# Conv, Fourier mixing and FFN on one core: merged reordering transfers, a depthwise unit on VectorE, packed sums over h

## Chip, core and metric

One core of a Trainium2 chip runs the whole batch of 32 images in one launch. The metric is the device time in microseconds; the profile is one execution of the same program. TensorE (PE) multiplies, VectorE (DVE), ScalarE (ACT) and GpSimd (POOL) do elementwise work, and SyncE (SP) issues every DMA of the steady state.

## Reference

For each of 32 images `x` (56 x 56 pixels, 96 channels, f32):

```python
# layer 0: an inverted bottleneck whose weights are mixed per image from four experts
rw = sigmoid(mean(x, (1, 2)) @ Wr + br)                      # 4 mixing weights of this image
h = relu(bn(x @ (rw . Wpw) + rw @ bpw))                      # 96 -> 384 channels
h = relu(bn(sum_e rw[e] * (depthwise3x3(h, Wdw[e]) + bdw[e])))
x = bn(h @ (rw . Wpwl) + rw @ bpwl) + x                      # 384 -> 96, shortcut
# layer 1, on tokens t = x as (3136, 96)
h = relu(bn(layernorm(t) @ w1.T))                            # 96 -> 192
X = fft(h, axis=tokens, norm="ortho")                        # over all 3136 tokens
y = ifft(relu(X.re*rd - X.im*id + rb) + 1j*relu(X.im*rd + X.re*id + ib)).real
t = t + bn(y @ w2.T)
t = t + ffn(layernorm(t))       # 96 -> 384 -> 96, operands in 8 bits (e5m2), sums in f16
```

## The kernel before

**Work of an image.** An image lives in two half tiles `xh[0]`, `xh[1]` (96 channels plus a row of ones, 30 rows w of 58), each in a ring of three places. Stages, with the names that the profile uses:

- *Mixing.* ACT sums each half; `pooled`, a small matmul with `wr_s` and a sigmoid give `mix`. DVE then mixes `wk` (expansion), `small` (depthwise taps and biases) and `wkc` (projection). `wkc` goes through DRAM (`wd`) into `wk2`, which has every fourth channel in each 32-partition quadrant.
- *Conv.* A half has three units of 128 channels, so an image has six. In a unit the depthwise 3x3 runs on PE in 32x32 tiles: pixels are split by parity, four parities and 8 channels make 32 rows, and a 32x32 matrix from `wg` (built by POOL) has the taps. Four groups g of 32 channels are expanded (4 matmuls `ps<-x,wk` each, one per pixel parity), ACT writes each group with a ReLU to `h`, and four DMAs `hp<-h` per group put channel and parity in the order that the tiles want: 16 DMAs of 54.4 KB per unit. The conv itself is 64 matmuls `ps<-hp,wg` on 16 tiles; ACT adds the bias, four DMAs `h<-hp` of 196 KB reorder back, and the projection (16 matmuls `ps<-h,wk` per unit, 32 rows each) ends with DVE adding to `xh`.
- *Fourier, forward.* Strips of 14 rows: transposes and `bn_stats` for the layernorm (`ln`), the matmul with `w1c` (`ps<-w1c,x`), the scaling `ha` on DVE, and the sums over h, `ps<-ha,da`: for each of 7 row pairs one matmul of 116 x 116 x 192. The two rows of a pair lie 58 partitions apart, and the matrix `da` (loaded for each strip, two DMAs of 178 KB) is half zeros: each row meets its own 58 columns only. ACT copies the result to `g`, two DMAs write it to DRAM `gd`.
- *Fourier, middle and back.* After all four strips, seven groups of frequencies: load `g2` (shown as `g<-gd`), transform over w (`ps<-dftb_s,g`), the complex ReLU on ACT and DVE (`za`, `zb`, `tmp`), `w2` (`ps<-w2a,za`, `ps<-w2b,zb`), the inverse over w (`ps<-zo,dftc_s`), `y`, and out to DRAM `yd`. Then per strip `yt` and `dd` are loaded and summed back over h (`ps<-dd,yt`).
- *FFN.* Per strip: layernorm in 8 bits (`nt`, turned with `pick8`: `ps<-pick,nt`), `fw1`, `fw2`, the sum into `xh`, and four DMAs per image to the output.

**Order.** Every steady-state instruction is first recorded as an `Op` with an engine, an estimated duration, a due time and the buffers that it reads, writes or takes. `Plan.order` plays these through, engine by engine, and emits them in that order; on the chip each engine keeps it. The due times repeat by `PERIOD`. Three images overlap: one in the conv, one in the Fourier stage, one behind it. Durations and lags of the plan are constants of the code, not measurements.

All instructions of the steady state go through one wrapper, `Pinned.issue`, so the profile shows them with one line, L261 before. They are told apart by their tiles.

Of the kernel before, what the change touches and what calls it, by code (L numbers as in the profile page):

```python
# [18 lines left out]
NE = 4  # L19
# [10 lines left out]
TP = 2 * (S + 2)  # L30
# [7 lines left out]
NG = 12  # L38
NSTK = 9 * NC3 + 2 * NC3 + 1
# [97 lines left out]
class Op:  # L137
    __slots__ = ("eng", "dur", "due", "emit", "bufs", "takes", "left", "ready", "after", "end", "seq")
# [3 lines left out]
LAG = {"PE": 0.25, "DVE": 0.12, "ACT": 0.2, "POOL": 0.2, "SP": 2.3}  # L142
SAME = {"PE": 0.0, "DVE": 0.06, "ACT": 0.05, "POOL": 0.05, "SP": 2.3}


class Plan:
# [5 lines left out]
    def add(self, eng, dur, due, emit, reads=(), writes=(), takes=()):  # L152
        op = Op()
        op.eng, op.dur, op.due, op.emit = eng, dur, due, emit
        op.takes = list(takes)
# [25 lines left out]
    def order(self):  # L181
# [3 lines left out]
        events, n = [], 0  # L185
        done = []
# [10 lines left out]
        def start(op, now):  # L197
            for b in op.takes:
                b.got = b.ring.take(b.n)
            op.end = now + op.dur  # L200
            free[op.eng] = op.end
            done.append(op)
            push(op.end, "end", op)
# [20 lines left out]
        while events:  # L224
            now = events[0][0]
            while events and events[0][0] <= now:
# [3 lines left out]
                elif kind == "end":  # L230
                    for a in x.after:
                        a.left -= 1
                        lag = SAME[x.eng] if a.eng == x.eng else LAG[x.eng]
                        a.ready = max(a.ready, now + lag)
                        if a.left == 0:
                            push(a.ready, "ready", a)
                    push(now + (2.3 if x.eng == "SP" else 0.15), "give", x)
                else:
                    for b in x.bufs:
                        b.users -= 1  # L240
                        if b.users == 0:
                            b.ring.give(b.got)
# [24 lines left out]
def kernel(  # L267
# [35 lines left out]
    xr = [ring(3, [C + 1, HW + 2, S + 2], F32, f"x{h}_") for h in range(2)]  # L303
# [26 lines left out]
    stk16 = const([128, NE + 1, 16 * NG + NG + 1], F32, "stk16")  # L330
# [11 lines left out]
    for p in range(2):  # L342
        nc.vector.tensor_copy(pick8[:, S * p : S * p + S], ident[:TP, (S + 2) * p : (S + 2) * p + S], saturate=False)
# [25 lines left out]

    with tc.tile_pool(name="prep", bufs=1) as pp:  # L370
# [8 lines left out]
        nc.vector.tensor_reduce(of_pixel, half.rearrange("p (r s) -> p s r", s=4), AX.X, ALU.add)  # L379
        raw = temp([128, 4, 27 * NE], "raw")  # L380
# [13 lines left out]
        for q in range(4):  # L394
            nc.sync.dma_start(rawb[q::4], stk[:, 30:33, :].rearrange("(g r) k e -> g r (k e)", r=4))
            nc.sync.dma_start(v2b[q::4], vecs[:, lo : lo + 12].rearrange("(g r) k -> g r k", r=4))
        row_s = temp([128, NROWS], "row_s")
# [19 lines left out]
        nc.sync.dma_start(dftb_s, dftb)  # L417
# [40 lines left out]
        bn_scale(s2b, v2b[:, :, 0:3], v2b[:, :, 9:12], EPS_CONV)  # L458
        s3 = temp([128, 1], "s3")
# [38 lines left out]
        bn_shift(stk16[:, NE, 17 * NG : 17 * NG + 1], vec("b3"), vec("m3"), s3, "sh3")  # L498

# [42 lines left out]
    r_h = places(4, [128, 15 * (S // 2 + 1)], F32, "h")  # L542
    r_hp = places(3, [128, 4, 15 * (S // 2 + 1)], F32, "hp")
# [3 lines left out]
    r_small = places(2, [128, 17 * NG + 1], F32, "small")  # L547
    r_mix = places(2, [128, NE + 4], F32, "mix")
    r_ones = places(2, [C, 128], F32, "pooled")
    r_wkc = places(1, [128, NC3, C], F32, "wkc")  # L550
    r_wk2 = places(1, [128, 4, NC3, C], F32, "wk2_")
    r_da = places(2, [TP, SQ, PA], F32, "da")
# [4 lines left out]
    r_g = places(2, [PA, 4, CH], F32, "g")  # L557
# [3 lines left out]
    r_tmp = places(4, [128, 5, 2, S], F32, "tmp")  # L561
# [9 lines left out]
    r_gd = ring(2, [PA, NQ, CH], F32, "gd", dram)  # L571
# [7 lines left out]
    add = plan.add  # L579
# [10 lines left out]
    PERIOD = 130.0  # L590

    def tokens(xb, w):
        at = w * (S + 2) + 1
        return xb.ap[0:C].rearrange("c w h -> c (w h)")[:, at : at + TP]

    def record(b):
# [6 lines left out]
        for h in range(2):  # L603
# [3 lines left out]
            else:  # L607
                add(
                    "SP", 3.0, t0 - 40, lambda h=h: x_dma(sy, b, h),
# [40 lines left out]
        def mix_wk2():  # L650
# [17 lines left out]
        add(  # L668
            "SP", 0.3, t0 + 8, lambda: sy.dma_start(wd.ap, wkc.ap.rearrange("p c o -> p (c o)")),
            reads=[(wkc, 0)], writes=[(wd, 0)], takes=[wd],  # L670
        )
        for s in range(4):
            add(
                "SP", 0.3, t0 + 12,
# [7 lines left out]

        for h in range(2):
            hid = [Buf(r_h2) for _ in range(NC3)]
            for c in range(NC3):
                due = t0 + (h * NC3 + c) * PERIOD / (2 * NC3)
                wg, hp = Buf(r_wg), Buf(r_hp)

                def weights(c=c, wg=wg):
                    shape = [128, 16, 8, 4]  # L690
                    m = mask.rearrange("p (t c q) -> p t c q", t=1, q=1).to_broadcast(shape)
                    t = small.ap[:, 64 * c : 64 * c + 64].rearrange("p (t c q) -> p t c q", c=1, q=4)
                    po.tensor_tensor(
                        wg.ap.rearrange("p g k (c q) -> p (g k) c q", q=4), m, t.to_broadcast(shape), ALU.mult
                    )

                add("POOL", 1.1, due - 12, weights, reads=[(small, 0)], writes=[(wg, 0)], takes=[wg])
                for g in range(4):
                    hg, ps = Buf(r_h), Buf(banks)
                    at = due - 10 + g * PERIOD / (8 * NC3)  # L700
                    chan = 128 * c + 32 * g

                    def expand(h=h, ps=ps, chan=chan):
                        for s in range(4):
                            pw, ph = divmod(s, 2)
                            te.matmul(
                                ps.bank()[32 * s : 32 * s + 32, 0:435],
                                wk.ap[:, chan : chan + 32],
                                xh[h].ap[:, pw : pw + 29 : 2, ph : ph + 57 : 2],
                                start=True, stop=True,  # L710
                            )

                    add(
                        "PE", 0.95, at, expand, reads=[(wk, 0), *((xh[h], k) for k in (0, 1, 2))],
                        writes=[(ps, 0)], takes=[ps, hg],
                    )
                    add(
                        "ACT", cols("ACT", 435), at + 1,
                        lambda ps=ps, hg=hg: se.activation(hg.ap, ps.bank()[:, 0:435], AF.Relu),
                        reads=[(ps, 0)], writes=[(hg, 0)],  # L720
                    )
                    for r in range(4):
                        add(
                            "SP", 0.1, at + 2,
                            lambda g=g, r=r, hg=hg, hp=hp: sy.dma_start(
                                hp.ap[32 * r : 32 * r + 32, g, :], hg.ap[r::4, :]
                            ),
                            reads=[(hg, 0)], writes=[(hp, (g, r))], takes=[hp] if g == r == 0 else [],
                        )
                ps = Buf(banks, 4)  # L730

                def conv(wg=wg, hp=hp, ps=ps):
                    for k in range(4):
                        bw, bh = divmod(k, 2)
                        for r in range(4):
                            at = slice(32 * r, 32 * r + 32)
                            for g in range(4):
                                te.matmul(
                                    ps.bank(r)[32 * g : 32 * g + 32, 0:TH],
                                    wg.ap[at, g, k, :],  # L740
                                    hp.ap[at, g].rearrange("p (w h) -> p w h", w=15)[:, bw : bw + 14, bh : bh + 28],
                                    start=(k == 0), stop=(k == 3),
                                )

                add(
                    "PE", 2.9, due, conv,
                    reads=[(wg, 0), *((hp, (g, r)) for g in range(4) for r in range(4))],
                    writes=[(ps, r) for r in range(4)], takes=[ps],
                )
                for r in range(4):  # L750
                    add(
                        "ACT", cols("ACT", TH), due + 1,
                        lambda c=c, r=r, ps=ps, hp=hp: se.activation(
                            hp.ap.rearrange("p g n -> p (g n)")[:, TH * r : TH * r + TH], ps.bank(r)[:, 0:TH], AF.Relu,
                            bias=small.ap[:, 16 * NG + 4 * c + r : 16 * NG + 4 * c + r + 1],
                        ),
                        reads=[(ps, r), (small, 0)],
                        writes=[(hp, ("out", r)), *((hp, (g, k)) for g in range(4) for k in range(4))],
                    )
                for q in range(4):  # L760
                    add(
                        "SP", 0.1, due + 3,
                        lambda q=q, hp=hp, to=hid[c]: sy.dma_start(
                            to.ap[32 * q : 32 * q + 32].rearrange("p r n -> p (r n)"),
# [531 lines left out]
```

## Time and profile before

| | |
|---|---|
| median of 3 runs | 5353.63 us (5351.17 to 5355.15) |
| the profiled execution | 5352.85 us |
| its span, first to last instruction | 5351.1 us |
| granted TensorE clock, mean | 0.924 |
| pitch of images (start of `pooled`, 956 to 5001 us) | 161.8 us |
| first expanding matmul | 66.9 us |
| DMA per image | 24 MB, 30 thousand packets |

In a line of groups, `ps<-hp,wg 32*32 32x392 f32 x24576 | 1068.8, 596 | 303.7 <-DMA hp<-h 282.9` means: matmuls that write PSUM from `hp` with weights `wg`, on a tile of 32 x 32, 32 partitions of 392 f32 elements, 24576 of them; busy 1068.8 us in all, 596 ns each; the engine idled 303.7 us before them, most of it until a DMA into `hp` landed. An f32 matmul of the code is two instructions on PE. Matmuls on different tiles of the array overlap, so one's duration is no measure of the rate; where that matters the text takes the step from one start to the next. PEclk is the granted clock in tenths of the full one.

### The profile page before, as it was taken

What the parts mean: (1) busy time and instruction counts of PE and PEld (TensorE: products, weight loads), DVE (VectorE), ACT (ScalarE), POOL (GpSimd) and SP (SyncE); (2) the same over time, 40 slices, a digit from 0 to 9 for tenths busy, and PEclk for the clock granted to TensorE, in tenths of its full rate; (3) what the DMA queues carried; (4) which work ended last, traced back from release to release, by engine and by line L of the source; (5) the groups of instructions that cost most, each with busy time, mean ns of one, the idle gap of its engine ahead of it and who ended that gap; (6) DMA issues with size and microseconds to landing.
All of it is one profiled execution on the core that took longest, in us unless ns stands there. A gap on an engine that the chain in (4) does not pass through costs nothing.

```text
span 5351.1 us, 133311 instructions
## 1 busy us (share of the span) xinstructions
PE 4688.6 (88%) x52802; PEld 2974.9 (56%) x52802; DVE 2612.8 (49%) x8867; ACT 2305.4 (43%) x4618; POOL 1210.3 (23%) x1236
## 2 busy tenths in 40 slices
PE   3898898989898899998889988898988898988986
PEld 1555555555565565555555555565555555655665
DVE  3244554454554454554454544454544444544545
ACT  2234443444543344544344543444544444434443
POOL 1111222222222222222222222122222122221223
PEclk8898999999999999999999999999999899999987
DMA  5666666666666666666666666666666666666652
GB/s 110 136 144 134 141 154 141 154 153 148 150 154 144 149 150 150 149 154 144 151 152 148 148 153 141 150 150 152 145 148 146 148 143 141 153 140 153 148 126 74
DMA packets 964628, 771.78 MB, mean 144 GB/s; under 512 B 654594, under 2 KB 861250, under 8 KB 964002
## 3 DMA queue, kind: packets, MB, share of 16 engines
q1 hardware_dynamic: 964002, 763.25, 63.8%
q8 instruction: 415, 6.80, 0.6%
q14 instruction: 211, 1.73, 0.1%
HBM read 274.71 MB, written 162.99 MB: 82 GB/s over the span
## 4 chain that ended last, share of the span: by engine, by line
PE 51%; DMA 15%; DVE 10%; SPq 6%; ACT 5%; issue 2%; POOL 1%; ACTq 0%; POOLq 0%; DVEq 0%
PE ps L261 51%; DMA hp<-h 7%; SPq L261 6%; DVE ln L261 4%; DMA h<-hp 2%; DVE nt L261 2%; ACT h L261 2%; DVE tmp L261 1%; ACT tmp L261 1%; DVE za L261 1%; DMA x<-in_x_dram 1%; POOL ln L261 1%; DMA da<-in_dfta_dram 1%; DMA out_dram<-x 1%; DMA gd<-g 1%
## 5 line engine op out<-in xcount | busy, mean ns | idle before, releaser
L261 PE MATMUL ps<-hp,wg 32*32 32x392 f32 x24576 | 1068.8, 596 | 303.7 <-DMA hp<-h 282.9
L261 PEld LDWEIGHTS ps<-hp,wg 32*32 32x32 f32 x24576 | 547.2, 113 | 774.5 <-DMA hp<-h 505.9
L261 ACT ACTIVATE hp<-ps,small 128x392 f32<-128x392 f32 x768 | 409.6, 588 | 1177.3 <-PE ps L261 1177.3
L261 PE MATMUL ps<-x,wk 97*32 97x435 f32 x6144 | 731.2, 574 | 46.2 <-ACT n L261 25.4
L261 POOL TENSOR_TENSOR wg<-mask,small 128x512 f32<-128x512 f32 x192 | 205.5, 1070 | 2202.2 <-PE ps L261 2012.7
L261 ACT ACTIVATE h<-ps 128x435 f32<-128x435 f32 x768 | 409.0, 533 | 567.7 <-PE ps L261 504.0
L261 PE MATMUL ps<-h,wk 32*96 32x392 f32 x6144 | 564.0, 495 | 2.0 <-DMA h<-hp 1.2
L261 DVE TENSOR_SCALAR h<-h,fb 128x784 f16<-128x784 f16 x384 | 177.5, 469 | 777.1 <-ACT h L261 775.9
L261 DVE SCALAR_TENSOR_TENSOR x<-ps,small,x 96x392 f32<-96x392 f32 x256 | 148.5, 622 | 728.0 <-PE ps L261 728.0
L261 POOL CAST h<-h 128x784 fp8e5<-128x784 f16 x384 | 328.2, 859 | 581.4 <-DVE h L261 581.4
L261 PEld LDWEIGHTS ps<-h,wk 32*96 32x96 f32 x6144 | 286.9, 158 | 253.2 <-issue 202.4
L261 PE MATMUL ps<-dftb_s,g 112*128 112x112 f32 x2816 | 412.1, 285 | 12.7 <-DMA g<-gd 12.2
L261 PEld LDWEIGHTS ps<-dftb_s,g 112*128 112x128 f32 x2816 | 365.6, 195 | 96.3 <-issue 77.6
L261 ACT CAST h<-ps 128x784 f16<-128x784 f32 x384 | 305.5, 815 | 241.4 <-PE ps L261 235.9
L261 PE MATMUL ps<-ha,da 116*116 116x192 f32 x1792 | 396.6, 376 | 7.7 <-ACT tmp L261 6.4
L261 POOL TENSOR_TENSOR ln<-ln,mhalf 116x7 f32<-116x7 f32 x256 | 394.3, 1540 | 21.3
L261 PEld LDWEIGHTS ps<-ha,da 116*116 116x116 f32 x1792 | 346.2, 210 | 68.8 <-ACT g L261 28.6
L261 PE MATMUL ps<-w1c,x 96*116 96x192 f32 x1792 | 334.1, 330 | 11.6 <-ACT h L261 11.5
L261 DVE BATCH_NORM_STATS2 ln<-ps 116x6 f32<-116x96 f32 x1792 | 315.7, 249 | 41.0 <-PE ps L261 41.0
L261 DVE SCALAR_TENSOR_TENSOR ha<-ps,ln,nshift 116x192 f32<-116x192 f32 x896 | 307.9, 409 | 33.9 <-POOL ln L261 33.3
L261 DVE TENSOR_SCALAR nt<-ps,ln 116x96 fp8e5<-116x96 f32 x896 | 267.0, 370 | 100.9 <-POOL ln L261 100.9
L261 PEld LDWEIGHTS <-fw 128*96 128x96 fp8e5 (+1 forms) x1536 | 151.3, 112 | 281.2 <-issue 233.3
(152 smaller groups left out, 6301.1 us busy)
## 6 DMA issues: line engine op xcount, KB each, us to landing
hp<-h SPq DMA_DIRECT2D x3072, 54.4 KB
h<-hp SPq DMA_DIRECT2D x768, 196.0 KB
da<-in_dfta_dram SPq DMA_DIRECT2D x256, 177.6 KB
dd<-in_dftd_dram SPq DMA_DIRECT2D x128, 355.2 KB
gd<-g SPq DMA_DIRECT2D x128, 336.0 KB
g<-gd SPq DMA_DIRECT2D x192, 224.0 KB
x<-in_x_dram SPq DMA_DIRECT2D x64, 609.0 KB
yt<-yd SPq DMA_DIRECT2D x128, 294.0 KB
```

The lines of the kernel that those rows point to most:

```text
L261: return self.tc.keep_in_program_order(method(*args, **kwargs))
```

## The change

1. **Transfers merged by unit.** `h` becomes a tile of a whole unit (four groups side by side; two places instead of four smaller ones), and four DMAs of 223 KB per unit take the place of sixteen `hp<-h`. The ring of `hp` has two places instead of three. All four groups must be ready before the first DMA, and the conv waits for all four DMAs.
2. **One of six units on VectorE** (half 0, chunk 2). Its channels are expanded 128 at a time (4 matmuls over 1740 columns), ACT applies the ReLU into `hv` and starts the accumulator with the middle tap and the bias, DVE adds the other eight taps (8 `scalar_tensor_tensor` of 128x784 on each of two quarter images, so 16 in all), ACT ends with a ReLU. No DMA, no `wg`. Its projection is 4 matmuls of 128 rows with `wkc`, which gets a second place.
3. **Sums over h in 64x64 tiles.** The two rows of a pair now lie 64 partitions apart (rows of `xh` are 64 wide), and `da` keeps only the 58 used columns, 64 apart. Four row pairs are 16 half-size problems, 8 matmuls on four tiles per group of up to four pairs; a group of three computes one pair twice. The packed matrix `dad` is made once at the start, on DVE from `dfta`, and lies in DRAM; a strip loads 91 KB twice from it. `gd` has another layout.
4. **The plan.** A DMA is now an issue of 0.45 us on SP and a transfer with its size on a shared queue (1.7 us and 0.22 MB per us); `PERIOD` is 125 instead of 130; some durations differ (conv 2.9 to 4.3). Every engine's order comes out new.

```diff
-LAG = {"PE": 0.25, "DVE": 0.12, "ACT": 0.2, "POOL": 0.2, "SP": 2.3}
+LAG = {"PE": 0.25, "DVE": 0.12, "ACT": 0.2, "POOL": 0.2, "SP": 0.2}
+DMA_LAG, DMA_RATE = 1.7, 2.2e5
...
+    def move(self, size, due, emit, **keys):
+        return self.add("SP", 0.45, due, emit, size=size, **keys)
...
+            if op.eng == "SP" and op.size:
+                nonlocal moved
+                moved = max(moved, op.end + DMA_LAG) + op.size / DMA_RATE
+                push(moved, "end", op)
...
-    r_h = places(4, [128, 15 * (S // 2 + 1)], F32, "h")
-    r_hp = places(3, [128, 4, 15 * (S // 2 + 1)], F32, "hp")
+    r_h = places(2, [128, 4 * 15 * HWP], F32, "h")
+    r_hp = places(2, [128, 4, 15 * HWP], F32, "hp")
-    r_wkc = places(1, [128, NC3, C], F32, "wkc")
-    r_da = places(2, [TP, SQ, PA], F32, "da")
+    r_wkc = places(2, [128, NC3, C], F32, "wkc")
+    r_da = places(2, [128, SQ, 64], F32, "da")
...
-    PERIOD = 130.0
+    PERIOD = 125.0
+    BY_VECTOR = ((0, DC),)
...
+        def by_vector(h, c, due, acc):
+            hv = Buf(r_h)
+            edges = (0, 8, 16, 23, 30)
...
+                    te.matmul(
+                        ps.bank()[:, 0 : n * (S + 2)], wk.ap[:, 128 * c : 128 * c + 128],
+                        xh[h].ap[:, edges[i] : edges[i + 1], 0 : S + 2], start=True, stop=True,
+                    )
...
+            def first(i):
+                src, to, w = taps(i, 4)
+                se.activation(to, src, AF.Identity, scale=w, bias=small.ap[:, NSM + 9 : NSM + 10])
+            def one(i, tap):
+                src, to, w = taps(i, tap)
+                ve.scalar_tensor_tensor(to, src, w, to, ALU.mult, ALU.add)
+            def last(i):
+                to = taps(i, 4)[1]
+                se.activation(to, to, AF.Relu)
...
-                    for r in range(4):
-                        add(
-                            "SP", 0.1, at + 2,
-                            lambda g=g, r=r, hg=hg, hp=hp: sy.dma_start(
-                                hp.ap[32 * r : 32 * r + 32, g, :], hg.ap[r::4, :]
+            for r in range(4):
+                move(
+                    223000, due - 10,
+                    lambda r=r: sy.dma_start(
+                        hp.ap[32 * r : 32 * r + 32].rearrange("p g n -> p (g n)"), hg.ap[r::4, :]
...
-                    "PE", 2.9, due, conv,
+                "PE", 4.3, due, conv, reads=[(wg, 0), *((hp, r) for r in range(4))],
...
+                if plain[c]:
+                    v = hid[c].ap.rearrange("p r n -> p (r n)").rearrange("p (w h) -> p w h", h=S)
+                    for q in range(4):
+                        qw, qh = pixel(q)
+                        te.matmul(
+                            ps.bank(q)[0:C, 0:TH], wkc.ap[:, c, :], v[:, qw::2, qh::2], start=False, stop=True,
+                        )
...
-                        da.ap[(S + 2) * p : (S + 2) * p + S], dfta[S * p : S * p + S, st * SQ : st * SQ + SQ, :]
+                        da.ap[XW * p : XW * p + S, :, 0:KR], dad[S * p : S * p + S, st * SQ : st * SQ + SQ, :]
...
-                    for q in range(nq):
-                        te.matmul(
-                            ps.pair[:PA, 256 * q : 256 * q + CH], da.ap[:, q0 + q, :],
-                            ha.ap[:, q, :], start=True, stop=True,
-                        )
+                    for t in range(2):
+                        for j in range(2):
+                            q = min(2 * t + j, nq - 1)
+                            for p in range(2):
+                                at = slice(XW * p, XW * p + S)
+                                te.matmul(
+                                    ps.pair[64 * j : 64 * j + 64, 512 * p + 256 * t : 512 * p + 256 * t + CH],
+                                    da.ap[at, q0 + q, :], ha.ap[at, q, :], start=True, stop=True,
+                                )
...
+        for i in range(2):
+            nc.sync.dma_start(big, dfta[:, i * (NQ // 2) : (i + 1) * (NQ // 2)])
+            for q in range(NQ // 2):
+                nc.vector.tensor_scalar_mul(to[:, q], v[:, q, :, 0], par[:PB, 0:1])
+                nc.vector.scalar_tensor_tensor(to[:, q], v[:, q, :, 1], par[:PB, 1:2], to[:, q], ALU.mult, ALU.add)
+            nc.sync.dma_start(dad[:, i * (NQ // 2) : (i + 1) * (NQ // 2)], small_a)
```

## The prediction

> **What bounds the kernel now.** I read the page's first three parts, then the waits, then one conv unit in the timeline, then the steady stretch by windows.
>
> ```profile
> PE 4688.6 (88%) x52802; PEld 2974.9 (56%) x52802; DVE 2612.8 (49%) x8867; ACT 2305.4 (43%) x4618; POOL 1210.3 (23%) x1236
> ...
> q1 hardware_dynamic: 964002, 763.25, 63.8%
> ...
> L261 PE MATMUL ps<-hp,wg 32*32 32x392 f32 x24576 | 1068.8, 596 | 303.7 <-DMA hp<-h 282.9
> ...
> L261 PE MATMUL ps<-ha,da 116*116 116x192 f32 x1792 | 396.6, 376 | 7.7 <-ACT tmp L261 6.4
> ```
>
> TensorE (PE) is the bound: 88% busy, the others at half or less, and 51% of the chain that ended last. Its largest group, the conv, is also the one it waits for longest: 303.7 us before it, 282.9 of them for the transfers `hp<-h`.
>
> ```profile
> 2588.79 6.71 SPq L261 DMA_DIRECT2D hp<-h  x8
> 2589.38 0.85 PE L261 MATMUL ps<-hp,wg 32*32 32x392 f32 x6
> 2595.25 2.60 PE L261 MATMUL ps<-hp,wg 32*32 32x392 f32 x39 [5.02 <-DMA hp<-h]
> ```
>
> This timeline shows such a wait: the conv starts, stops after 6 matmuls, and stands 5.02 us until pieces of `hp` land, while the DMA-issuing queue (SPq) spends 6.71 us on eight issues. One `hp<-h` issue takes 592 ns at the median and there are 3072; all DMA issues together take 3566 us of SPq, 111 us per image.
>
> ```profile
> 956.00:5001.00 4045.00, 3627.76 (x41258) 2295.41 (x41255) 2008.43 (x6803) 1797.89 (x3602) 935.32 (x950) 0.93 0.66 148
> ```
>
> The columns are the window, busy PE, PEld, DVE, ACT, POOL, clock, DMA share, GB/s. It holds 25 image pitches (starts of `pooled`, 956 to 5001 us): **161.8 us per image**, of which PE is busy 145.1. The clock is 0.93 because PE runs at half clock for 813 us of the span, in spells of 3.4 to 10 us that begin in or just behind the longer PE gaps (the 5.02 us gap above lies in one of 6.8 us). A stall is paid twice: as idle time, and as half speed after it.
>
> The profiled execution took 5352.85 us, its span 5351.1; the median of the runs is 5353.63, so the sum needs no rescaling.
>
> **The change, part by part, per image.** The dependences can be followed in the order of instructions of both kernels. I counted the PE work that the order puts between two points, at undisturbed durations of this trace.
>
> *One unit leaves the conv.* An undisturbed unit takes 3.66 us of PE (5th percentile of 192): −3.7. Its 16 expanding matmuls (3.6 us) become 4 over 1740 columns in all. A full-array f32 row steps 163 ns per 192 columns (`ps<-w1c,x`), two instructions a matmul: 1740 × 0.85 ns × 2 = 3.0, −0.6. Its projection is 4 full matmuls instead of 16 quarter ones: 8 × 333 = 2.7 against 2.9, taken as 0. Sum −4.2.
>
> *The other five units stop waiting.* From a conv instruction to the next PE instruction the steps add up to 41.8 per image; six undisturbed units are 22.0. So 19.8 are stall and half clock. In the order of before, the PE work between a unit's last expanding matmul and its conv is 5.5, 6.9, 3.0, 10.2, 4.6 and 6.8 us; in the changed order 12.9, 7.0, 12.8, 11.6 and 11.0. The need: four issues replace sixteen, the data is 891 KB in packets of 6960 B, which the trace lacks. Nearest is `h<-hp`, 803 KB in 6272 B packets on the same 32-partition pattern: 5.5 us (median) from first to last packet, the first 1.1 us after the issue. Scaled: 0.55 (ACT) + 0.6 + 1.1 + 6.1 = 8.4 us on a free queue. Four of five units are covered with 2.6 to 4.5 us to spare, one is 1.4 short. I leave 3 of the 19.8 and book −16.8; bounds −10 (queueing eats the spare) and −19.8.
>
> Merging does not make the bytes cheaper. A 1740 B packet took 93 ns on the mean, a 6272 B one 589: 18.6 against 10.6 B/ns. The five merged units send 5 × 128 × 32 = 20480 packets in the run; at 650 ns (589 scaled by bytes) over 16 engines that is 832 us, where all six units now cost 574. `h<-hp` loses a sixth of 905 (−151), `da` becomes 100352 packets of 232 B at about 21 ns (132) instead of 14336 of 3248 B at 197 (176), and 2560 fewer DMAs save some 34 of closing 4 B writes. Together +30 on 3450 us: DMA work stays at 108 to 109 us per image.
>
> The rows give 146 GB/s for such a group (803 KB in 5.5 us), and they are used. The Trainium skill is of two minds here ("SBUF — State Buffer"): its section The DMA setup-cost knee wants the largest single transfer, its section Door 1: The DMA port swizzle says that 32 partitions reach half the ports, some 218 GB/s at best. By the page 891 KB would take 4.1 us and a fixed 2, an estimate; that would spare the short unit 1 us and leave the sum 1 us per image lower.
>
> *SPq.* 120 issues of 0.6 us become 40: 111 falls to about 60 us per image. It is what lets SPq be on time; counted in the wait above.
>
> *Sums over h.* 56 instructions at 172 ns are 9.7, with half clock 11.7 (steps per image). After: 4 strips × 16 matmuls × 2 = 128 instructions on 64x64 tiles. If four tiles run at once (32x96 row tiles do: 78 ns per 392-column instruction, where one alone takes 327), 41 ns each: 5.2. Gain −6.0. If they do not overlap, 128 × 163 = 20.9: +9.2. The first is nearer to three other tiled groups here.
>
> *VectorE (DVE).* 16 multiply-adds of 128x784. The rows `small<-stk,mix,small` (205 columns, 434 ns) and `wk<-wpw_s,mix,wk` (384, 619) rise by 1.03 ns per column; carried on from `wk`, 784 columns take 1.03 us, and from `tmp<-za,tmp` (224, 385 ns) 0.96: 16.0 us per image. DVE goes from 80.3 to 96.3 of the pitch and is still not the bound. The order leaves 51.6 us of PE work between this unit's expansion and its projection; hidden. But DVE is in order, and each new step can hold up the normalization behind it, for which PE waits today (79.8 us before `ps<-pick,nt`, 38.5 before `ps<-w2b,zb`, 3.7 per image). One step more in front of such a wait is 1 us; I book +3, bounds 0 and +8.
>
> ```profile
> L261 DVE SCALAR_TENSOR_TENSOR tmp<-za,tmp x224: 374/385/1764, 247.5 to 5281.1; 128x224 f32<-128x224 f32 x96, 128x280 f32<-128x280 f32 x16
> ```
>
> Minimum, median, maximum: a 385 ns step has stretched to 1764, and 90 of the 224 began while a POOL instruction ran (539 ns on the mean). POOL is busy 37 us per image, so of 16 steps some five meet it, at 0.15 to 0.3 us: about 1 us on DVE, inside the +3. If each of five stretched like the longest row (1.38 us over the median) it would be 7, inside the upper bound. The Trainium skill names a cause that speaks against this part ("SBUF — State Buffer", Who interferes with whom): a DVE instruction with two inputs in SBUF and a GpSimd one that reads SBUF exclude each other for a whole instruction. By it every meeting would cost half a POOL instruction or more, which the mean of 539 ns does not show.
>
> *Shorter covers.* From the last backward transform over q to the first over h the order left 12.8 us of PE work, now 8.3, for a DVE copy (0.57), an issue, `yd`, another issue, `yt`; PE waits 11.3 us in all for it now. I book +1 (0 to +3). Conv to projection gains (5 to 9.4), and needs 2.4 (ACT) + 1.1 + 5.5: +0.5.
>
> *ACT* gains 1.0 (5.5 us for the new unit against 4.5) and 0.7 (copies of `g` always 768 wide) on 72: at half load, nothing. *Half clock elsewhere*: fewer spells, −1.5.
>
> *Preparation.* The matrix of the sums is packed on DVE: 56 steps of 58 columns, about 0.2 us (`stk<-wide,s2f` has 173 ns), 11 us ahead of the first mixing step, with a second load behind the first half and a few more loads: +18 once (10 to 30).
>
> **Sum.** 161.8 − 4.2 − 16.8 − 6.0 + 3 + 1.5 − 1.5 = **137.8 us per image**. 24.0 × 31 images (the last one drains on latencies) = 744; 5353 − 744 + 18 = 4627, rounded to **4625 us**. As a check: the PE steps in the order, all undisturbed, add to 121.8 before and 114.0 after, so 40.0 us per image are lost today and 23.8 in the forecast.
>
> **The rivals.**
> *The DMA queue becomes the bound.* 109 us of packets in 138 is 79%, against 66% now, and one queue serves all in turn. If the 6960 B packets take the 785 ns that 6272 B ones take in the middle of a burst (20480 × 785 / 16 = 1005 us instead of 832), it is 114 us, and half the conv stall remains. Pitch about 148: 4930. Against it: the order puts most transfers 10 us ahead.
> *The tiles do not overlap*, so the packed matrix does not do what it says: 137.8 + 15.2 = 153, about 5100.
> *DVE sets the pace*: its lock at the upper bound and chain waits of 8: 144, about 4810.
> *Slower than before.* `hp` has two places instead of three, and a conv needs the whole unit. If landings take so long that every conv waits, nothing hides it. Break-even is 24 us per image back, 4.8 per unit beyond what is booked: landing 16 us behind the last expanding matmul, twice the 8.4. With 20 it is 5 × 9 = 45: pitch 180, some 5950 us. Needed is a queue that is nearly full; 79% speaks against it.
>
> **How the numbers follow.** Forecast 0.62, DMA bound 0.15, DVE 0.10, tiles 0.06, slower 0.06, no difference 0.01. Runs spread by under 0.1%; about 0.2% is what a measurement can tell from no change. Faster 0.93, same 0.01, slower 0.06. The low end takes the conv stall wholly away, no DVE price and two more us of half clock away: 130, 4385. The high end reaches the DMA case: 4920.
>
> **What would show it.** Right: idle time before `ps<-hp,wg` under 100 us and its busy time near 160 × 4 = 640 us; clock above 0.95; `ps<-ha,da` 64x192 below 220 us; DVE near 3130 us busy; DMA share near 80%; first expanding matmul near 85 us. Wrong: conv waits on `hp<-h` above 200 us (queue), `ps<-ha,da` above 500 us (tiles), new long waits of PE on DVE `nt` or `zb` (DVE order), or a pitch that none of these explains.

## The result: slower by 4.6%

| | before | after |
|---|---|---|
| median of 4 runs | 5352.77 us (5351.17 to 5355.15) | 5599.41 us (5594.63 to 5606.10) |
| the profiled execution, its span | 5352.85, 5351.1 us | 5596.55, 5594.7 us |
| granted TensorE clock, mean | 0.924 | 0.88 |
| pitch of images 5 to 25 (starts of `pooled`) | 160.9 us | 169.1 us |
| PE at half clock | 813 us | 1345 us |

The ratio is 1.0461, with a 95% interval from 1.0443 to 1.0479. The forecast was 4625 us, with a range up to 4920: the kernel was to become faster, and it became slower.

These are the lines of the page after that answer to those shown of before, with the vector unit's steps and the sums over h (groups: busy us, mean ns of one | idle us before them and what ended it).

```profile
PE 4414.9 (79%) x49474; PEld 2762.0 (49%) x49474; DVE 3122.6 (56%) x9445; ACT 2338.2 (42%) x4619; POOL 1197.0 (21%) x1204
...
q1 hardware_dynamic: 946154, 687.80, 63.6%
...
PE 47%; DMA 26%; DVE 12%; ACT 7%; issue 3%; SPq 3%; POOL 2%; ACTq 0%; POOLq 0%; DVEq 0%
...
L277 PE MATMUL ps<-hp,wg 32*32 32x392 f32 x20480 | 887.4, 653 | 597.5 <-DMA hp<-h 595.6
...
L277 DVE SCALAR_TENSOR_TENSOR h<-h,small,h 128x784 f32<-128x784 f32 x512 | 514.7, 1045 | 41.0 <-ACT h L277 38.1
```

PE is less busy than before, in a longer span: the work did get less. The conv has fewer matmuls and waits twice as long for `hp<-h` (597.5 us against 303.7), and a quarter of the chain is now DMA. And yet the queue's share, 63.6% of 16 engines, is what it was before. By the page DMA has a third of its time to spare.

The chain of waits in one stretch of the profile after (start, length, what) shows where it stands:

```profile
2741.78 0.68 issue
2742.46 0.65 ACT h L277
2743.11 9.20 DMA hp<-h
2752.45 7.81 PE ps L277 x128
...
2763.50 15.67 PE ps L277 x133
2779.38 13.83 DMA hp<-h
2793.25 8.94 PE ps L277 x128
```

For two convs in a row the chain runs through 9.20 and 13.83 us of transfer, from the first issue to the landing; PE stands idle for 6.76 and 13.05 us of them. SP's own timeline, for the time before the second wait:

```profile
2762.07 3.13 SPq L277 DMA_DIRECT2D h<-hp  x4
2765.30 0.54 SPq L277 DMA_DIRECT2D out_dram<-x  x1
2765.94 8.21 SPq L277 DMA_DIRECT2D gd<-g  x4
2774.24 3.15 SPq L277 DMA_DIRECT2D da<-dad  x2
2777.48 1.81 SPq L277 DMA_DIRECT2D dd<-in_dftd_dram  x1
2779.38 3.36 SPq L277 DMA_DIRECT2D hp<-h  x4
```

Four issues of `gd<-g` hold SP for 8.21 us, and the issues of `hp<-h` stand behind them in order: ScalarE had finished writing `h` at 2766.83 us, 12.5 us before the first of them. One line of the tile `g` in each kernel, before and then after (minimum/median/maximum ns of an issue), shows that long issues of `gd<-g` are the rule:

```profile
L261 SPq DMA_DIRECT2D gd<-g x512: 239/318/1683, 161.2 to 5224.1; - x171
```

```profile
L277 SPq DMA_DIRECT2D gd<-g x512: 227/1510/5007, 165.9 to 5456.9; - x171
```

The same number of issues became almost five times as long at the median. Part of that is their shape: half of the issues of before write only four rows, and 512 issues of 64 rows (e1 below) have a median of 625 ns. The prediction has no term for this transfer.

### The profile page after: what moved, and what is told of

Read it like the earlier page. It is cut to its first block, busy times and chain, and to the rows that moved or that the text cites. A ratio compares the mean times of both kernels' runs of the same rounds, so it can differ in the third digit from the quotient of the medians.

```text
span 5594.7 us, 122771 instructions
## 1 busy us (share of the span) xinstructions
PE 4414.9 (79%) x49474; PEld 2762.0 (49%) x49474; DVE 3122.6 (56%) x9445; ACT 2338.2 (42%) x4619; POOL 1197.0 (21%) x1204
## 3 DMA queue, kind: packets, MB, share of 16 engines
q1 hardware_dynamic: 946154, 687.80, 63.6%
## 4 chain that ended last, share of the span: by engine, by line
PE 47%; DMA 26%; DVE 12%; ACT 7%; issue 3%; SPq 3%; POOL 2%; ACTq 0%; POOLq 0%; DVEq 0%
PE ps L277 47%; DMA hp<-h 13%; DMA g<-gd 4%; DMA out_dram<-x 4%; DVE h L277 3%; DVE ln L277 3%; DMA x<-in_x_dram 2%; SPq L277 2%; POOL ln L277 2%; DVE x L277 1%; DMA dd<-in_dftd_dram 1%; ACT h L277 1%; DMA gd<-g 1%; ACT tmpa L277 1%; DVE ha L277 1%
## 5 line engine op out<-in xcount | busy, mean ns | idle before, releaser
L277 PE MATMUL ps<-hp,wg 32*32 32x392 f32 x20480 | 887.4, 653 | 597.5 <-DMA hp<-h 595.6
L277 PE MATMUL ps<-x,wk 97*32 97x435 f32 (+2 forms) x5376 | 708.9, 586 | 22.7 <-DVE tmpa L277 14.9
L277 DVE SCALAR_TENSOR_TENSOR h<-h,small,h 128x784 f32<-128x784 f32 x512 | 514.7, 1045 | 41.0 <-ACT h L277 38.1
L277 ACT ACTIVATE h<-ps 128x435 f32<-128x435 f32 (+2 forms) x768 | 400.1, 539 | 240.0 <-PE ps L277 211.6
L277 POOL TENSOR_TENSOR ln<-ln,mhalf 120x7 f32<-120x7 f32 x256 | 390.3, 1525 | 21.3
L277 PE MATMUL ps<-w1c,x 96*120 96x192 f32 x1792 | 352.7, 338 | 29.7 <-ACT h L277 21.6
L277 DVE TENSOR_SCALAR nt<-ps,ln 120x96 fp8e5<-120x96 f32 x896 | 267.2, 372 | 175.4 <-POOL ln L277 174.3
L277 DVE SCALAR_TENSOR_TENSOR ha<-ps,ln,nshift 120x192 f32<-120x192 f32 x896 | 310.6, 411 | 82.2 <-PE ps L277 50.3
L277 ACT ACTIVATE tmpa<-ps,fa 128x224 f32<-128x224 f32 (+1 forms) x448 | 223.3, 498 | 256.5 <-PE ps L277 208.7
L277 PEld LDWEIGHTS ps<-w1c,x 96*120 96x120 f32 x1792 | 288.9, 187 | 82.1 <-ACT h L277 41.7
L277 DVE BATCH_NORM_STATS2 ln<-ps 120x6 f32<-120x96 f32 x1792 | 319.1, 253 | 9.7 <-PE ps L277 9.5
```

The source lines that it names most:

```text
L277: return self.tc.keep_in_program_order(method(*args, **kwargs))
```

## The theories

**A: two engines.** The change to `gd` (part 3 of the change) also alters the shape of the write. Before, `gd<-g` was cut into 112 and 4 partitions; after, each write covers the 58 used columns, `g.ap[64 * j : 64 * j + KR]`. The packet records of the trace have no engine number, but they have starts and ends. Counted from them, the time in which so many packets of `gd<-g` were under way (e1 to e3 are the experiments below):

| kernel (packet size) | 1 at once | 2 | 3 | 4 and more |
|---|---|---|---|---|
| after, 58 partitions (1536 B) | 223 us | 1382 | 172 | 6 |
| e1, 64 partitions (1536 B) | 72 us | 34 | 18 | 359, of it 249 at 12 to 17 |
| e2, 58 partitions (3072 and 2304 B) | 414 us | 1419 | 84 | 1 |
| e3, 29 partitions (1536 B) | 3038 us | 196 | 0 | 1 |

So a write of 58 rows goes out on two engines, one of 29 on one, one of 64 on all sixteen (ends are modelled, hence a few more at once than there are engines). 52064 packets of 67.8 ns on two engines are 52064 × 67.8 / 2 = 1765 us each. All packets together are 3592 us per engine on the mean, of which `gd<-g` is 221; the rest, 3371, comes on top if it is even: 5136 us on these two engines, 92% of the span, where the mean over 16 says 63.6%. This is an estimate, and a low one, since the rest is not even. The loads of `dd` have 116 rows, and in before and in e1 their packets are four at a time for most of their time (473 us and 478 us; more than five for under 5). Their 169 us on the mean are then 675 on each of four engines. If the two are among these, they carry some 5640 us, the whole span.

The same count speaks for it: after, the packets of `dd` are two at a time for 372 us, where before has 30 and e1 38, so two of the four lag behind. Taking packets of all kinds, after has one or two under way for 951 us, e1 for 238. A transfer that is spread over all engines, `hp<-h` above all, ends when its part on those two has ended.

The Trainium skill states the rule ("DMA: Bandwidth & Descriptors", Why a DMA increments its semaphore by 16 and not by 1): a DMA is shared out over the largest number of engines up to 16 that divides the size of its slowest dimension on both sides, and for a DMA that SyncE issues they are the lowest-numbered ones. The table agrees: 58 is 2 × 29, 29 is prime, 64 is 4 × 16. The numbers of the two engines the records don't show; that `dd` lags on two of its four fits their always being the same.

**B: merging and order.** Four large issues that need a whole unit, two places of `hp` and a new plan make the conv late, with or without `gd<-g`; this is the rival "Slower than before" of the prediction by itself.

## Experiments

**e1: 64 rows.** The write covers 64 partitions, six of them unused, and moves 10% more bytes.

```diff
-    r_gd = ring(2, [KR, S, CH], F32, "gd", dram)
+    r_gd = ring(2, [64, S, CH], F32, "gd", dram)
...
-                            g.ap[64 * j : 64 * j + KR, 0:nt].rearrange("k t p m -> k t (p m)"),
+                            g.ap[64 * j : 64 * j + 64, 0:nt].rearrange("k t p m -> k t (p m)"),
```

> The changed kernel, with the writes of g to DRAM on 64 partitions instead of 58 (six rows of zeros more; gd gets 64 rows). Order, number of DMA issues and everything else are the same. Theory A (two engines: a DMA over 58 partitions runs on 2 of the 16 DMA engines, 58 = 2 x 29, and these two, with 1765 us of gd packets each besides an even share of 211 us per 1/16 of the rest, are full): over 16 engines the packets cost about 243 us each, SP's issues of gd<-g fall from 1.78 us on the mean back to 0.35, the conv's waits for hp<-h fall from 597 us to under 150, and the time is what the forecast had, 4600 to 4800 us. Theory B (the merged unit transfers, with two places of hp, or the new order themselves make the conv wait): unchanged within 2%, 5500 to 5650 us.

4770.99 us (4760.48 to 4779.07); 0.8936 of before, 0.8918 to 0.8954. From the page of e1, and its line of `gd<-g`:

```profile
PE 4266.3 (89%) x49474; PEld 2673.2 (56%) x49474; DVE 3118.7 (65%) x9445; ACT 2340.3 (49%) x4619; POOL 1194.7 (25%) x1204
...
q1 hardware_dynamic: 958698, 696.08, 78.2%
...
L277 PE MATMUL ps<-hp,wg 32*32 32x392 f32 x20480 | 754.0, 553 | 55.7 <-DMA hp<-h 49.6
...
L277 SPq DMA_DIRECT2D gd<-g x512: 473/625/5361, 167.0 to 4642.7; - x171
```

This takes 828 us away from after (5599.41). The wait for `hp<-h` falls from 595.6 to 49.6 us, with merging, plan and two places as they were: B does not explain the slowdown. The share of the queue rises to 78.2%. Even this mean hides a difference: by the count above the four engines that carry `dd` have 4252 us of packets, 89% of the span.

**e2: before, with 58.** The kernel before, its write cut 58 | 58.

```diff
-                for a, z in ((0, PB), (PB, PA)):
+                for a, z in ((0, 58), (58, PA)):
...
-        gd_parts = [(gd, (st * SQ + q0, a)) for st in range(NS) for q0 in (0, 4) for a in (0, PB)]
+        gd_parts = [(gd, (st * SQ + q0, a)) for st in range(NS) for q0 in (0, 4) for a in (0, 58)]
```

> The kernel before, with each write of g to DRAM cut at 58 | 58 partitions instead of 112 | 4. Same bytes, same number of issues, same order, nothing merged. Theory A: 29696 packets at 128 ns on two engines are 1900 us each on top of about 3210 us of the rest, 5110 us in all, 95% of the span before: slower, 5500 to 6000 us, and the conv waits longer for hp<-h. Theory B: within 1% of 5353 us, since nothing is merged.

6251.98 us (6236.20 to 6255.53), 1.1706 of before (1.1684 to 1.1727): the spread alone makes the old kernel 17% slower, more than the 5500 to 6000 us expected. From its page:

```profile
q1 hardware_dynamic: 959906, 763.24, 53.5%
...
L261 PE MATMUL ps<-hp,wg 32*32 32x392 f32 x24576 | 1252.7, 663 | 978.1 <-DMA hp<-h 960.8
```

It has the same number of bytes as before, and more than three times the wait for `hp<-h`. Two engines carry 1756 us of `gd<-g` and 3157 of the rest, 4913 of 6234 (79%); with `dd` on four engines it is 5373 (86%). So load alone does not set this time. The issues of `gd<-g` are hardly longer here, 0.40 us on the mean against 0.34 before, so their length is not needed for the loss. What the trace shows instead is SP standing still: 540 us in 275 waits for landings of `gd<-g`, where before has 8.2 us in 8. SP issues in order, so all issues behind such a wait are late, those of `hp<-h` too. How much of the 17% that is, no run separates.

**e3: 29 rows.** After, each write cut in two of 29 rows.

```diff
-                        lambda j=j, nt=nt, at=at, g=g: sy.dma_start(
...
+                        lambda j=j, nt=nt, at=at, g=g: [
+                            sy.dma_start(
...
+                                g.ap[64 * j + a : 64 * j + a + 29, 0:nt].rearrange("k t p m -> k t (p m)"),
+                            )
+                            for a in (0, 29)
+                        ],
```

> The changed kernel, with each write of g cut into two of 29 partitions (same bytes, 16 more issues per image). Theory A: 29 is prime, so each runs on one engine; that engine has 52064 packets x 68 ns = 3530 us of gd besides its share of 3371 us: at least 6900 us. A theory in which the number of engines does not matter: 5600 to 5750 us, for the extra issues.

7054.81 us in one run. One engine carries 3437 us of `gd<-g` and some 3489 of the rest if that is even: 6926 of 7053, 98% (with `dd` on four engines 7426, over the span, so such sums are good to some 5%: packets of one engine overlap a little, as the second column of the table shows). For 2340 us a single packet is under way in the whole core, in e1 for 179. Here one engine sets the time of the whole kernel, while the page shows little more than half:

```profile
q1 hardware_dynamic: 946154, 687.80, 52.0%
...
L277 PE MATMUL ps<-hp,wg 32*32 32x392 f32 x20480 | 862.4, 644 | 1308.2 <-DMA hp<-h 1305.6
```

**e1b: 48 and 10 rows.** No padding, two DMAs, by the rule on 16 and 10 engines.

```diff
-                        lambda j=j, nt=nt, at=at, g=g: sy.dma_start(
...
+                        lambda j=j, nt=nt, at=at, g=g: [
+                            sy.dma_start(
...
+                                g.ap[64 * j + a : 64 * j + z, 0:nt].rearrange("k t p m -> k t (p m)"),
+                            )
+                            for a, z in ((0, 48), (48, KR))
+                        ],
```

> The changed kernel with each write of g cut at 48 | 10 rows: the same 58 rows and bytes as there, no padding, 16 issues more per image at 0.3 us. 48 rows can use 16 engines, 10 rows ten. Theory A (number of engines): near e1_pad64, 4760 to 4900 us. If what helped in e1_pad64 was the other layout of gd (64 rows) or the padding, it stays near 5600 us.

4927.62 us (4903.05 to 4939.72), 0.9196 (0.916 to 0.9232). With the bytes of after it gains 672 us where e1 gains 828, so e1's gain is not one of padding. It misses the upper end of what was expected by 28 us and stays 157 us behind e1. That is not SP's time: its issues take 74.5 us per image, in e1 73.6, although there are 16 more. The packets of 6960 B take 697 ns here and 650 in e1, and the wait for `hp<-h` is 172.1 us; why, no run shows.

**e4: no unit on VectorE**, otherwise e1.

```diff
-    BY_VECTOR = ((0, DC),)
+    BY_VECTOR = ()
```

> e1_pad64 without the VectorE unit: all six units run on TensorE again, BY_VECTOR is empty. If the unit on VectorE is worth what the sum had (4.2 us of PE per image and a sixth of the conv waits, less 3 us of DVE holdups), this is slower than e1_pad64 by 2 to 7 us per image, 60 to 220 us. If the 16 DVE steps hold up the rest more than they save, it is faster than e1_pad64.

5180.29 us (5173.74 to 5185.67), 0.9707 (0.9689 to 0.9725). The unit on DVE is worth 409 us, 12.8 per image, about twice the upper end of what was expected. Without it PE at half clock rises from 502 to 836 us, PE's idle time before the conv from 1.7 to 5.3 us per image, and packets from 3766 to 4161 us per engine; by the prediction's prices only 4.2 of the 12.8 are undisturbed PE work.

**e5: matrices loaded for the first image only**, otherwise e1. From the second image on, strips use matrices of another strip.

```diff
-                    lambda p=p, st=st, da=da: sy.dma_start(
+                    lambda p=p, st=st, da=da: b == 0 and sy.dma_start(
...
-                364000, due - 6, lambda st=st, dd=dd: sy.dma_start(dd.ap, dftd[:, st * SQ : st * SQ + SQ, :]),
+                364000, due - 6, lambda st=st, dd=dd: b == 0 and sy.dma_start(dd.ap, dftd[:, st * SQ : st * SQ + SQ, :]),
```

> e1_pad64 in which only the first image loads da and dd; later images use what lies there (so the sums over h use another strip's matrix). Order and everything else are the same. It takes 131 + 169 = 300 us per engine of packets and 12 issues per image away, and no work from any other engine. Theory D (with the two-engine writes gone, the DMA queue with its 78% is the next bound): the time falls by about as much, to 4450 to 4600 us. Theory P (TensorE is the bound again): it falls by less than 60 us, 4710 to 4770 us.

4633.69 us (4617.81 to 4665.95), 0.8672 (0.863 to 0.8713): 137 us less, which lies between the two expectations. The loads take 278 us of packets per engine with them; others grew, so that the sum falls by 241 (3766 to 3525). If the queue alone were the bound, about as much would have come off. From its page:

```profile
PE 4183.7 (91%) x49474; PEld 2630.2 (57%) x49474; DVE 3118.6 (68%) x9445; ACT 2342.6 (51%) x4619; POOL 1195.7 (26%) x1204
...
q1 hardware_dynamic: 843130, 628.40, 75.5%
```

With the spread put right, PE is the busiest engine, and DMA adds to its time by coming late. The edit also takes issues from SP (73.6 to 60.9 us per image) and the load that lies on four engines, so which of these the 137 us come from is not shown.

**e6: merged writes of `h`, split transfers**, otherwise e1. Each `hp<-h` is cut into its four groups at the same place in SP's order.

```diff
-                    lambda r=r: sy.dma_start(
-                        hp.ap[32 * r : 32 * r + 32].rearrange("p g n -> p (g n)"), hg.ap[r::4, :]
-                    ),
+                    lambda r=r: [
+                        sy.dma_start(hp.ap[32 * r : 32 * r + 32, g, :], hg.ap[r::4, 435 * g : 435 * g + 435])
+                        for g in range(4)
+                    ],
```

> e1_pad64 with each merged hp<-h cut into its four groups again (packets of 1740 B instead of 6960 B, 60 issues more per image at 0.6 us, so SPq 74 -> 110 us per image of 149), all issued where the merged one is, so the conv still waits for the whole unit. If bytes cost less in small packets (93 ns per 1740 B against 612 ns per 6960 B, 300 us per engine less) and this counts, it is faster: 4500 to 4650 us. If merging pays by its fewer issues, it is slower: 4850 to 5100 us. If neither counts, within 1%.

5030.11 us (5022.83 to 5051.10), 0.94 (0.9377 to 0.9423). Its page:

```profile
q1 hardware_dynamic: 1050858, 696.20, 62.5%
...
L277 PE MATMUL ps<-hp,wg 32*32 32x392 f32 x20480 | 1004.8, 607 | 28.2 <-DMA hp<-h 22.1
...
L277 PEld LDWEIGHTS ps<-hp,wg 32*32 32x32 f32 x20480 | 434.6, 113 | 540.9 <-DMA hp<-h 232.2
```

The split packets are cheaper (82.4 ns per 1740 B, 422 us per engine; merged 649.8 ns per 6960 B, 832 us), the share falls from 78.2 to 62.5%, and the kernel is 259 us slower. Issues take 106 instead of 74 us of SP per image, and PE is at half clock for 915 us instead of 502. PE's idle time before conv matmuls is even shorter (28.2 us against 55.7), but the conv is busy for 1004.8 us instead of 754.0. A matmul is only 10% longer (607 against 553 ns). The waiting shows at the weight loads between them, which stand 232.2 us for `hp<-h`, in e1 84.4: the conv starts and then runs in pieces. So merging pays, at packets that cost twice as much per byte. That it pays by its fewer issues is the likely reading; the number of landings changes with them, and no run separates the two.

**e7: two units on VectorE**, otherwise e1.

```diff
-    BY_VECTOR = ((0, DC),)
+    BY_VECTOR = ((0, DC), (1, DC))
```

> e1_pad64 with a second unit on VectorE, chunk 2 of half 1. The first one was worth 409 us (e4_pad64_novec 5180, e1_pad64 4771). If the next one does the same work for PE and the DMA queue (some 380 us per engine of packets, 4 us of PE per image), 4360 to 4500 us; DVE would be at 3634 us. If DVE, in order and near 80%, now holds PE up, 4771 us or more.

4887.25 us (4872.88 to 4914.75), 0.9133 (0.9102 to 0.9164): the second unit costs 116 us where the first brought 409.

```profile
PE 4167.5 (85%) x43842; PEld 2694.6 (55%) x43842; DVE 3680.1 (75%) x9957; ACT 2420.1 (49%) x4619; POOL 1452.5 (30%) x1172
...
L277 DVE SCALAR_TENSOR_TENSOR h<-h,small,h 128x784 f32<-128x784 f32 x1024 | 1057.9, 1059 | 39.0 <-ACT h L277 32.0
...
L277 PE MATMUL ps<-dd,yt 116*96 116x112 f32 x1792 | 245.6, 300 | 184.6 <-DMA dd<-in_dftd_dram 75.6
```

No engine is full, and PE idles 21.2 us per image instead of 13.6. The largest part is new and stands before `ps<-dd,yt` (5.8 per image): most of it waits for landings of `dd` and `yt` (75.6 and 61.6 of 184.6 us). PE's waits for DVE results grow too, for `pooled` from 30.7 to 97.8 us, for `ha` from 21.7 to 89.1, for `nt` from 32.2 to 48.5. The latter are the "DVE order" case of the prediction, one unit later than feared; it is not the whole loss.

**e8: the plan's period**, otherwise e1: `PERIOD` 118 and 135 in place of 125.

> e1_pad64 with due times 118 us apart instead of 125, so a new order of all engines. If the order is only a tie-break, within 1% of e1_pad64 (4723 to 4819 us). If it matters as much as the parts of the change, it moves by more, in either direction.

> e1_pad64 with due times 135 us apart, nearer to the pitch of 144 us that e1_pad64 has. Same expectation: within 1% if the order is only a tie-break; faster if due times near the true pitch place the loads better, slower if later due times leave PE less to choose from.

118 gives 4739.18 us (4732.95 to 4775.21), 0.8873 (0.8836 to 0.8909), 0.7% under e1 and the fastest here that computes all of the reference. 135 gives 4973.58 us (4964.64 to 4977.69), 0.9295 (0.9276 to 0.9313), 4.2% over e1, with 274.6 us of waits for `hp<-h`. So the order is more than a tie-break. All three plans space the images closer than the chip then runs them (pitch 142.9, 144.0 and 150.4 us for 118, 125 and 135); why the third order is so much worse is not shown.

## Why the prediction was wrong

**The step that failed** is the end of the part on the conv: "Together +30 on 3450 us: DMA work stays at 108 to 109 us per image." It sums packets over 16 engines as if every DMA were spread over all of them, and it does not list `gd<-g` among the changed transfers at all; the write was read as "another layout". Measured, the mean moved by 142 us (3450 to 3592 per engine), which the mean share of 63.6% could have borne, but 1765 us of `gd<-g` lie on two engines, which then carry 5136 or more. In e1, which differs in the spread and six rows of padding, the pitch is 144.0 us; with 58 rows it is 169.1. So this step is worth 25.1 us per image, and all else together missed by 144.0 − 137.8 = 6.2.

**The rival that came true** is "Slower than before", by its own break-even. It asked for a landing 16 us behind the last expanding matmul; from the end of the last ACT of a unit to the last packet of `hp` the mean over the units is 15.8 us after (7.7 to 27.8 by unit), and 10.9 in e1, where 8.4 − 0.55 was booked. Of the 15.8 some 4.6 are SP not yet being at the first issue. "Needed is a queue that is nearly full; 79% speaks against it" was right in its first half; the share was the wrong measure. The sign shown as wrong, conv waits on `hp<-h` above 200 us, is there with 595.6.

**The other terms**, read in e1, where the two engines do not cover them:

- *Stall and half clock of the conv*: 3 us per image were left, 6.9 are (conv steps add up to 25.2, undisturbed units to 18.3). Its 55.7 us of idle time were forecast (under 100); its busy time was not (754.0 against 640). The term "−16.8" was −12.9. Of the 6.9 only 1.7 are idle time of PE; the rest is half clock and weight loads that wait for `hp<-h` (84.4 us in the run), not separated here.
- *Sums over h*: the tiles do run at once. A step from one instruction to the next is 37 ns undisturbed, so 128 make 4.7 us, a little under the forecast 5.2; as they ran, half clock included, they come to 8.3 per image, not 5.7. So −3.4 for −6.0. These two terms give 3.9 + 2.6 = 6.5, against the 6.2 that were missing; what else was off nearly cancels.

The line of that group in the profile after answers to the `ps<-ha,da` line of before: 4096 instructions of 347 ns on the mean, and only 236.0 us busy, so some six are under way at a time by these records.

```profile
L277 PE MATMUL ps<-ha,da 56*64 56x192 f32 x4096 | 236.0, 347 | 7.7 <-ACT g L277 3.9 <-DVE ha L277 2.2 <-issue 1.1
```

- *SPq*: 111 us per image were to become 60. It is 108.1 after, since most of what `hp<-h` gave up (63.7 to 18.8) went to `gd<-g` and `da` (9 to 40); 73.6 in e1.
- *VectorE*: 1045 ns a step and 3122.6 us in all, much as forecast (0.96 to 1.03, near 3130). What was missed is what the unit is worth: 12.8 us per image by e4, where −4.2 and +3 were booked. Part of its gain is the conv stall that a sixth unit would have (e4 has 3.6 us more idle time before the conv per image); the sum had that under another heading ("The other five units stop waiting").
- *VectorE and POOL*: the prediction read the mean of 539 ns as speaking against a full exclusion. That mean mixes two kinds. Of the 62 steps of `tmp<-za,tmp` that began while POOL ran `x<-x,y`, `wg` or `h<-h`, all but one ended a nearly fixed time behind POOL's instruction (241 to 307 ns); the 29 that began in POOL's work on `ln` took 376 ns on the mean, no longer than those that met no POOL instruction (386). After, 30 of the 512 long steps began during `wg`, and all ended 830 to 834 ns behind it, 1317 ns each on the mean instead of 1028. So a step that meets one of these does stand until POOL has ended, but it costs only 0.3 us per image.
- *Packets of 6960 B*: 612 ns each after and 650 in e1, the latter the value booked; the case with 785 ns did not come. (By the sum's own rule its pitch of 148 is 4943 us, not 4930, so the range up to 4920 did not quite reach it.)
- *Preparation*: the first `pooled` starts 21 us later (75.6 against 54.3), forecast 18.

The range failed with the step: its upper end was built from a queue with 114 us of packets in 148, evenly spread.

## What to carry to other kernels

When a change alters the partition range of a DMA, work out on how many engines it now lies, and sum DMA time for the fullest engine, not for the mean: here 58 rows took 5599 us and 64 took 4771. A wait on one transfer may be made by another: where the page's share leaves room and landings are late, look at the lengths of issues ahead of it on its queue, at what that queue itself waits for, and count packets under way by size. Merging transfers can pay even where the bytes get dearer (e6): the issuing queue works in order and is shared.

## What the runs showed of the hardware

- A write from 58 partitions keeps one to three packets under way, mostly two, one from 29 one or two, one from 64 mostly 12 to 17 by the records (after and e2, e3, e1). A load of 116 rows keeps four (`dd` in before and e1).
- Issues can get longer while such writes are outstanding: `gd<-g` takes 0.70 us on the mean in e1, 1.78 after and 2.13 in e3; `da<-dad`, issued near them, 0.61 in e1 and 1.42 after. In e2 they hardly do (0.40 us against 0.34 before); most of its issues give an engine half as many packets. That the issuing queue waits for room on the full engines is the likely reason; no run shows it by itself.
- Half clock goes with idle time of PE: in before, of its 111 idle gaps over 2 us, 109 lie in a spell at half clock or have one begin within 4 us. Spells last 3.4 to 20.5 us there. Their total grows with late work (404 us in e5, 502 in e1, 1345 after, 2883 in e3). Open: what starts those of e6, where 128 spells stand against 27 such gaps.
- Open: how the loss of e2 divides between its two engines (79 to 86% of the span) and SP's waits for `gd<-g`.
- Loading `da` and `dd` once for the whole run was not tried; e5 puts its gain at no more than about 137 us. Cutting the 116 rows of `dd` into 112 and 4, as `yt` is, was not tried either.
